# A four-layer sequence model on one Trainium2 core: layer 3 moved into the list scheduler, and bank-to-SBUF moves on whichever engine is free

## The chip, the core and the metric

The kernel runs on one core of one Trainium2 chip. The core has a matrix engine (PE, with its weight loads listed apart as PEld), three elementwise engines (DVE, ACT, POOL) and a sync engine (SP) that issues most DMAs. Each engine works through its own queue in order; the engines wait for each other by semaphores. On-chip data lie in SBUF; PE writes its results to PSUM, which has eight banks of 128 x 512 float32 values, and DVE or ACT read them from there. The metric is the device time of one execution in microseconds, lower being better.

## The reference, cut to what matters

A batch of two sequences of 1024 tokens with 256 features goes through four layers, each adding to x. Layer 0 is a linear attention. Layers 1 and 2 are state-space layers: layer 1 has one recurrence, layer 2 two (the second one runs over the reversed sequence). Layer 3 is a full softmax attention of 16 heads of 16 features.

```python
# layer 1 (layer 2 has two of these, the second on the flipped sequence)
dA  = exp(dt[:, :, None] * A)                  # 512 channels x 16 states
hst = hst * dA + (dt * x)[:, :, None] * B[:, None, :]
y   = einsum('bds,bs->bd', hst, C)
...
# layer 3
xn = layer_norm(x); q = xn @ q_w + q_b; k = xn @ k_w + k_b
att = softmax(einsum('bnhl,bmhl->bnmh', q, k) + (1 - mask) * -1e6, axis=2)
v = (xn @ v_w + v_b) * mask
y = einsum('bnmh,bmhl->bnhl', att, v)
h = layer_norm(y) * (1 + scale) + shift        # scale, shift from emb
return x + silu(h) @ out_w + out_b
```

## The kernel before, in words

**Layer 0** runs first, one batch after the other, with the framework's own scheduling. It is not changed, but for the pool of two small tiles.

**Layers 1 and 2** are made of twelve *halves*: 3 recurrences x 2 batches x 2 halves of 512 tokens. A half is 64 scans: 16 states x 4 blocks of 128 channels, numbered 64 * i + 4 * s + m. For each scan,

- ACT scales `dtuT` to `bxT` (line 774, `scaled`) and makes the decay `da` = exp(dt * a) (L788, `decay`);
- PE transposes four 128x128 blocks of `bxT` into a PSUM bank (L603 in `four`, called from `turned`);
- DVE runs the scan itself over `da` and that bank into `state` (L822, `scan`);
- POOL multiplies the state with a row `cb` spread over partitions (L854, `weighted_state`), into one of four `hc` buffers;
- PE transposes `hc` and sums it in four accumulation banks (L869, `summed`), which `drained` (L883) copies out at the end of a half, two on DVE and two on ACT.

Around the recurrences lie chains that prepare the next halves and finish the last: `before_1`, `step_sizes`, `between`, `before_2`, `after_1`, `after_2a`, `after_2b`, `joined`. They use PE products (`project` L608, `out_rows` L617), PSUM banks that they hold for some operations, and 42 SBUF buffers of 128x512 called `unit`.

Who comes next is not left to the framework in this stage. A *list scheduler* in Python (class `Order`) runs while the kernel is built. Each chain is a generator, a *part*, that yields "this operation takes engine X for so long, and needs these results". The scheduler keeps planned times of every engine, picks the operation that can start earliest (ties go by a place number `v`, the scan's number or a chain's own), and only then lets the part emit its instruction. Buffers come from *stores* in the same way: `stores.banks` holds four PSUM banks for transposes and chains (of which chains may hold two at a time, by two *tickets*), `stores.acc` the four accumulation banks, and each buffer carries the planned time from which it is free. The durations are constants in `act`, `vec`, `gps`, `turn`, `mat`. The order found in this way is the order of each engine's queue (`manual_schedule` over PE, ACT, DVE, POOL, SP). The semaphore waits are added by the framework, from what the emitted instructions read and write.

The eight PSUM banks are eight tiles before:

```python
tiles = [mm.tile([P, TH], F32, name=f"bank{i}") for i in range(8)]
stores.acc = Store(order, tiles[:4])
stores.banks = Store(order, tiles[4:])
```

**Layer 3** opens after the scheduler is done, with its own pools and with PE alone in a written order. It loads x3 from HBM (`x_sb`), which `after_2b` wrote, loads the weights, normalises and transposes (L264), makes V (L299) and q, k (L1283). Eight groups follow, each four heads of one batch. A group has two passes. The *first pass* (`maxima`) makes scores (L1301, 32-row matmuls into pairs of banks `s`) and takes negated row maxima on DVE (L1305), which are put into q (L1311 to L1321). The second (`weighted`) makes the transposed scores (L1360, into three banks `ps`), takes exp on ACT (L1365), and sums p times V on PE (L1330 into `av`); at the end of a half of the queries `av` is copied, turned and divided (L1337 to L1345). The first pass of group n + 1, the second of group n and the projections of group n + 2 are woven together in 16 steps per group (`together`). The first group's first pass and the last group's second pass run without a partner. `modulated_out` (norm, silu, output product) follows after each batch's last group.

Of the kernel before, what the change touches and what calls it, by code (L numbers as in the profile page):

```python
# [10 lines left out]
F32 = mybir.dt.float32  # L11
# [10 lines left out]
P = 128  # L22
B, T, D = 2, 1024, 256
NB = T // P
# [153 lines left out]
def blocks_kernel(ctx: ExitStack, tc: tile.TileContext, d: dict, out: bass.AP, offs: dict):  # L178
# [255 lines left out]
    def layer0(b):  # L434
# [60 lines left out]
        qmax = small.tile([P, nh], F32, name="qmax")  # L495
# [3 lines left out]
        qsum = small.tile([P, nh], F32, name="qsum")  # L499
# [44 lines left out]
    def act(*needs, n=1, v=None):  # L544
        return op(ACT, 0.6 * n, 0.6 * n + 0.2, *needs, v=v)
# [7 lines left out]
    def turn(*needs, v=None):  # L553
        return op(PE, 0.64, 0.85, *needs, v=v)

    def mat(n, *needs, v=None):
        return op(PE, 0.925 * n, 0.925 * n + 0.2, *needs, v=v)
# [29 lines left out]
    def free_units(bufs, at):  # L587
        for b in bufs:
            stores.units.put(b, at)

# [69 lines left out]
    def step_sizes(H, w_dbc, w_dt, t_u, v0):  # L660
# [42 lines left out]
        def sizes(m):  # L703
# [30 lines left out]
            t1 = yield act(t1, H.dtuT)  # L734
            nc.scalar.copy(
                H.dtuT.tile[:, :, m * P : (m + 1) * P], b.tile.rearrange("p (k e) -> p k e", k=4)
# [12 lines left out]
    def recurrences(halves):  # L749
# [131 lines left out]
        def drained(a, y, k, t):  # L881
            t = yield (vec if k % 2 else act)(a, y, t)
            (nc.vector.tensor_copy if k % 2 else nc.scalar.copy)(y.tile, a.tile)  # L883
            stores.acc.put(a, t)
# [46 lines left out]
    def before_1(H, b, h, carry, v0):  # L931
# [14 lines left out]
        for kb in range(2):  # L946
            p = yield from bank()
            t = yield turn(p, *ts)
            four(p.tile, lambda k: block_of(xg, k)[:, kb * P : (kb + 1) * P])
            t = yield act(t, hT[kb])  # L950
            nc.scalar.activation(
                hT[kb].tile, p.tile, AF.Identity, bias=bm[:, kb, b : b + 1], scale=wm[:, kb, b : b + 1]
            )
            free_bank(p, t)
# [4 lines left out]
        def convolved(m):  # L959
# [5 lines left out]
            t1 = yield act(t1, x)  # L965
            nc.scalar.copy(raw[:, 3:], p.tile)
            t1 = yield op(ACT, 0.3, 0.5, t1)
# [3 lines left out]
            else:  # L971
                nc.scalar.copy(raw[:, :3], carry[:, m, :])
            t1 = yield act(t1)
            nc.scalar.activation(
                p.tile, p.tile, AF.Identity, bias=col("conv_b", m), scale=cw(m, 3)
            )
# [9 lines left out]
        def gates():  # L986
            for m in range(NM):
# [3 lines left out]
                t1 = yield act(t1, z[m])  # L991
                nc.scalar.copy(z[m].tile, p.tile)
# [45 lines left out]
    def between(b, h, v0):  # L1038
# [46 lines left out]
        for kb in range(2):  # L1085
# [3 lines left out]
            t = yield act(t, xT[kb])  # L1089
            nc.scalar.activation(  # L1090
                xT[kb].tile, p.tile, AF.Identity, bias=col("norm2_b", kb), scale=col("norm2_g", kb)
# [6 lines left out]
        def activation():  # L1098
            z = yield get(stores.units, NM)
            for m in range(NM):  # L1100
# [3 lines left out]
                t1 = yield act(t1, z[m])  # L1104
                nc.scalar.activation(z[m].tile, p.tile, AF.Identity, bias=col("bx", m))
# [13 lines left out]
    def joined():  # L1119
# [5 lines left out]
        for i, name in enumerate(("w2b", "w2c")):  # L1125
# [4 lines left out]
            for m in range(2):  # L1130
# [7 lines left out]
                t2 = yield act(t2)  # L1138
                nc.scalar.copy(wz[:, i, m, :], b.tile)
# [18 lines left out]
    def before_2(H, b, i, h, v0):  # L1158
# [5 lines left out]
        for m in range(NM):  # L1164
# [3 lines left out]
            t = yield act(t, H.u[m])  # L1168
            u = H.u[m].tile
            nc.scalar.activation(  # L1170
                u[:, ::-1] if i else u, p.tile, AF.Identity,
                bias=bzc[:, i * NM + m : i * NM + m + 1],
# [24 lines left out]
    def after_2b(H, b, h, v0):  # L1197
# [39 lines left out]
        free_units(H.u, t1)  # L1237


    def attention_inputs(b):  # L1240


        xb = x_sb[:, b * NB : (b + 1) * NB, :]
        xn = work.tile([P, NB, D], F32, name="xn", tag="t8")
        layernorm(xn, xb, NB)
        xT = work.tile([P, 2, T], F32, name="xT", tag="t8")
        to_features(xn, affine(xT, lambda kb: col("norm_w", kb), lambda kb: col("norm_b", kb)))


        mrow = work.tile([1, T], F32, name="mrow3", bufs=1)  # L1250
        nc.scalar.dma_start(mrow, d["mask_rows"][1, b : b + 1, :])
        nc.vector.tensor_scalar(mrow, mrow, -1.0, 1.0, ALU.mult, ALU.add)
        nc.vector.tensor_scalar(mrow, mrow, -1e6, None, ALU.mult)
        mrow_d = dram.tile([1, T], F32, name="mrow_d")
        nc.sync.dma_start(mrow_d, mrow)

        vp = vps[b]

        def evac_v(t, ps):
            tmp = work.tile([P, 2, D], F32, name="res", bufs=2)  # L1260
            nc.vector.tensor_tensor(tmp, ps, over(bv3, 2), ALU.add)
            for j in range(2):
                c = (B + b) * NB + t + j
                nc.gpsimd.tensor_scalar(
                    vp[:, t + j, :, :HD3],
                    tmp[:, j, :].rearrange("p (h e) -> p h e", e=HD3),
                    mcols[:, c : c + 1], None, ALU.mult,
                )

        linear_t(view(w3b, 0, 2, D), xT, 2, evac_v)  # L1270
        y = work.tile([P, NB, D], F32, name="y3", bufs=2)
        return xT, mrow_d, vp, y

    def queries_and_keys(xT, mrow_d, g, out):

        q = work.tile([P, T], F32, name="q3", bufs=3)
        k = work.tile([P, T], F32, name="k3", bufs=3)
        out.append((q, k))
        for dst, w, name in ((k, 2 * E, "k_b"), (q, 0, "q_b")):
            for h in range(2):  # L1280
                ps = mm.tile([P, TH], F32, name="ps")
                for kb in range(2):
                    nc.tensor.matmul(  # L1283
                        ps, lhsT=view(w3a, w, 2, E)[:, kb, g * P : (g + 1) * P],
                        rhs=xT[:, kb, half(h)], start=kb == 0, stop=kb == 1,
                    )
                nc.scalar.activation(dst[:, half(h)], ps, AF.Identity, bias=col(name, g))
                yield
        for j in range(4):
            r = 32 * j + HD3 + 1  # L1290
            nc.sync.dma_start(k[r : r + 1, :], mrow_d)

    def maxima(q, k, negm, half_max):

        for t in range(NB):
            for h in range(2):
                for jp in range(2):
                    s = scp.tile([P, 2, TH], F32, name="s")
                    for i in range(2):
                        r = slice(64 * jp + 32 * i, 64 * jp + 32 * i + 32)  # L1300
                        nc.tensor.matmul(  # L1301
                            s[:, i, :], lhsT=q[r, t * P : (t + 1) * P], rhs=k[r, half(h)],
                            start=True, stop=True,
                        )
                    nc.vector.tensor_reduce(  # L1305
                        half_max[:, h, t, 2 * jp : 2 * jp + 2], s, AX.X, ALU.max, negate=True
                    )
                    yield
            if t % 4 == 3:
                h, ts = t // 4, slice(t - 3, t + 1)  # L1310
                nc.vector.tensor_tensor(  # L1311
                    negm[:, ts, :, HD3], half_max[:, 0, ts, :], half_max[:, 1, ts, :], ALU.min
                )
                ps = mm.tile([P, TH], F32, name="ps")
                for i in range(4):
                    nc.tensor.transpose(
                        ps[:, i * P : (i + 1) * P],
# [400 lines left out]
```

## Time and profile before

| what | value |
|---|---|
| median of 3 runs | 2410.27 us (2406.91 to 2411.26) |
| profiled execution, its own time | 2412.0 us |
| profiled execution, span from first to last instruction | 2410.2 us |
| mean granted PE clock | 0.947 |
| PE busy | 2027.8 us, 84% of the span |
| DVE busy | 1626.6 us, 67% |
| ACT busy | 1620.8 us, 67% |
| POOL busy | 1167.9 us, 48% |
| first and last scan start | 296.8 and 1639.6 us |
| first score matmul of layer 3 | 1699.4 us |

The shares are averages over stages: layer 0 up to 297 us, the twelve halves up to 1641, layer 3 after that. So the profile is read stage by stage, with the table of busy times by stretch, and within a stage by what ended the idle time of an engine (the waits). A wait is written "engine tile line <- engine tile line: total us, times, longest". An engine's row "128x512 f32 x768 | 553.8, 725" is the number of instructions, their busy time together and the mean ns of one. Matmuls of float32 count twice or more in such rows, since one is issued as several passes; four 128x128 transposes make one "turn".

### The profile page before, as it was taken

To read this page: it belongs to the slowest core of one execution; us is meant where nothing else is said; L and a number is where in the kernel's file an instruction comes from. 1 tells how busy PE (TensorE), PEld (TensorE's weight loads), DVE (VectorE), ACT (ScalarE), POOL (GpSimd) and SP (SyncE) were. 2 spreads that over 40 slices of the span, in tenths; PEclk is the share of its full clock that TensorE was granted. 3 is DMA by queue.
4 is the path that set the end of the run, shared out by engine and by line. 5 is a ranking of instruction groups with operands and counts; after the bars stand their busy time and mean duration, and the time that the engine had idled before them with its cause. 6 is when DMAs were issued, how large, how long until landed. Compare 5 with 4: busy or idle time off the path is not lost.

```text
span 2410.2 us, 32499 instructions
## 1 busy us (share of the span) xinstructions
PE 2027.8 (84%) x11648; PEld 1237.1 (51%) x11648; DVE 1626.6 (67%) x1958; ACT 1620.8 (67%) x2738; POOL 1167.9 (48%) x1022
## 2 busy tenths in 40 slices
PE   5766788988888788887888888885899999899986
PEld 4555456666666566656666666664343233323322
DVE  2462368797978787988887897995655555555622
ACT  1223689798979799998897898982034454445544
POOL 1012259595978787979777797995110000000000
PEclk9887799999999999999999999997889999999989
DMA  5002122122212321223131211323000000000000
GB/s 224 0 18 70 40 50 67 58 61 62 80 62 68 82 55 53 71 54 110 58 93 50 62 47 55 86 65 124 1 1 1 1 1 1 18 1 1 1 1 18
DMA packets 119898, 118.71 MB, mean 49 GB/s; under 512 B 59348, under 2 KB 78164, under 8 KB 118840
## 3 DMA queue, kind: packets, MB, share of 16 engines
q1 hardware_dynamic: 116612, 109.63, 15.3%
q0 software_dynamic: 1536, 4.20, 0.5%
q10 hardware_dynamic: 1588, 2.80, 0.4%
q8 instruction: 92, 1.51, 0.3%
q14 instruction: 70, 0.57, 0.1%
HBM read 92.92 MB, written 23.47 MB: 48 GB/s over the span
## 4 chain that ended last, share of the span: by engine, by line
PE 37%; ACT 11%; DVE 8%; POOL 7%; issue 3%; DMA 1%; POOLq 0%; DVEq 0%; SPq 0%; ACTq 0%
PE ps L1360 9%; PE s L1301 7%; POOL hc L854 6%; PE av L1330 5%; DVE state L822 5%; ACT da L788 4%; ACT bxT L774 4%; PE ps L1283 3%; PE bank L869 3%; PE bank L603 2%; PE bank L608 2%; DVE half_max L1305 1%; PE bank L617 1%; PE ps L299 1%; PE bank L668 1%
## 5 line engine op out<-in xcount | busy, mean ns | idle before, releaser
L854 POOL TENSOR_TENSOR hc<-state,cb 128x512 f32<-128x512 f32 x768 | 959.5, 1282 | 236.9 <-DVE state L822 199.8
L869 PE MATMUL bank<-ident,hc 128*128 128x128 f32 x3072 | 496.8, 286 | 151.5 <-POOL hc L854 95.9
L788 ACT ACTIVATE da<-unit,a_neg 128x512 f32<-128x512 f32 x768 | 553.8, 725 | 61.6 <-DVE state L822 60.9
L774 ACT ACTIVATE bxT<-dtuT,bT 128x512 f32<-128x512 f32 x768 | 546.7, 724 | 16.3 <-PE bank L603 15.8
L822 DVE TENSOR_TENSOR_SCAN state<-da,last,bank 128x512 f32<-128x512 f32 x384 | 468.2, 1266 | 59.0 <-PE bank L603 44.1
L869 PEld LDWEIGHTS bank<-ident,hc 128*128 128x128 f32 x3072 | 339.3, 143 | 325.3 <-POOL hc L854 286.2
L822 DVE TENSOR_TENSOR_SCAN state<-da,bank 128x512 f32<-128x512 f32 x384 | 451.8, 1209 | 80.6 <-PE bank L603 34.9
L603 PE MATMUL bank<-ident,bxT 128*128 128x128 f32 x3072 | 464.3, 278 | 32.7 <-DVE state L822 24.4
L1305 DVE TENSOR_REDUCE half_max<-s 128x2 f32<-128x1024 f32 x256 | 303.1, 1220 | 214.6 <-PE ps L1360 185.4
L1365 ACT ACTIVATE p<-ps 128x512 f32<-128x512 f32 x512 | 278.8, 597 | 250.4 <-PE ps L1360 247.1
L603 PEld LDWEIGHTS bank<-ident,bxT 128*128 128x128 f32 x3072 | 361.5, 143 | 80.5 <-DVE state L822 43.5
L1360 PE MATMUL ps<-q,k 32*128 32x512 f32 x1024 | 365.3, 644 | 8.2 <-ACT p L1365 8.1
L319 POOL TENSOR_TENSOR x_sb<-x_sb,res 128x512 f32<-128x512 f32 x16 | 20.5, 1284 | 672.1 <-DVE res L317 672.1
L1301 PE MATMUL s<-k,q 32*128 32x512 f32 x1024 | 277.3, 655 | 8.0 <-DVE half_max L1305 7.8
L1360 PEld LDWEIGHTS ps<-q,k 32*128 32x128 f32 x1024 | 115.3, 186 | 137.7 <-ACT p L1365 98.4
L1301 PEld LDWEIGHTS s<-k,q 32*128 32x128 f32 x1024 | 90.2, 192 | 140.2 <-DVE half_max L1305 94.7
L1330 PE MATMUL av<-p,vp 128*32 128x512 f32 x1024 | 137.7, 615 | 0.0
L603 PE MATMUL bank<-ident,unit 128*128 128x128 f32 x448 | 74.4, 299 | 14.9 <-POOL unit L730 5.3
L730 POOL TENSOR_TENSOR unit<-unit,unit 128x512 f32<-128x512 f32 x48 | 61.2, 1276 | 33.0 <-DVE unit L726 33.0
L274 ACT ACTIVATE xT<-ps,cols 128x512 f32<-128x512 f32 x16 | 11.5, 775 | 92.9 <-PE ps L264 92.8
L1330 PEld LDWEIGHTS av<-p,vp 128*32 128x32 f32 x1024 | 21.2, 109 | 94.2 <-issue 93.3
L603 PEld LDWEIGHTS bank<-ident,unit 128*128 128x128 f32 x448 | 55.3, 152 | 27.3 <-POOL unit L730 8.2
(194 smaller groups left out, 1957.5 us busy)
## 6 DMA issues: line engine op xcount, KB each, us to landing
cb<-c_d SPq DMA_DIRECT2D x192, 256.0 KB
sz_d<-unit SPq DMA_DIRECT2D x16, 256.0 KB
unit<-sz_d SPq DMA_DIRECT2D x16, 256.0 KB
x_d<-unit SPq DMA_DIRECT2D x16, 256.0 KB
act_d<-unit SPq DMA_DIRECT2D x16, 256.0 KB
y_d<-unit SPq DMA_DIRECT2D x16, 256.0 KB
unit<-y_d SPq DMA_DIRECT2D x16, 256.0 KB
unit<-act_d SPq DMA_DIRECT2D x16, 256.0 KB
```

The source lines that it names most:

```text
L603: nc.tensor.transpose(ps[:, k * P : (k + 1) * P], src(k), ident)
L774: nc.scalar.activation(x.tile, H.dtuT.tile[:, k, :], AF.Identity, scale=H.bT.tile[:, k * 2 * NS + s : k * 2 * NS + s + 1],)
L788: nc.scalar.activation(x.tile, H.dt[m].tile, AF.Exp, scale=a_neg[:, H.n, m, s : s + 1])
L822: nc.vector.tensor_tensor_scan(st.tile[:, m % 2, :], da.tile, bx.tile, H.last[:, s, m : m + 1] if H.h else 0.0, ALU.mult, ALU.add,)
L854: nc.gpsimd.tensor_tensor(x.tile, st.tile[:, m % 2, :], c.tile, ALU.mult)
L869: nc.tensor.matmul(acc[k].tile[:, m * P : (m + 1) * P], lhsT=x.tile[:, k * P : (k + 1) * P], rhs=ident, is_transpose=True, start=s == 0 an ...
L1283: nc.tensor.matmul(ps, lhsT=view(w3a, w, 2, E)[:, kb, g * P : (g + 1) * P], rhs=xT[:, kb, half(h)], start=kb == 0, stop=kb == 1,)
L1301: nc.tensor.matmul(s[:, i, :], lhsT=q[r, t * P : (t + 1) * P], rhs=k[r, half(h)], start=True, stop=True,)
L1305: nc.vector.tensor_reduce(half_max[:, h, t, 2 * jp : 2 * jp + 2], s, AX.X, ALU.max, negate=True)
L1330: nc.tensor.matmul(av[32 * j : 32 * j + 32, :], lhsT=vp[:, t, 4 * g + j, :], rhs=p[j], start=t == 0, stop=t == NB - 1,)
L1360: nc.tensor.matmul(s, lhsT=k[r, t * P : (t + 1) * P], rhs=q[r, half(h)], start=True, stop=True,)
L1365: nc.scalar.activation(p[j], s, AF.Exp)
```

## The change

1. Layer 3 becomes parts of the scheduler: `keys_mask`, `attention_inputs`, `queries_and_keys`, `steps`, `sums_of`, `shift`, `finished`, `attention_out`. Batch 0's inputs and the first q and k have places in the last half (`step0 - 60`, `step0 - 40`, where `step0` = 768 is the place after the last scan). The steps themselves begin in `freed`, when the last half's accumulation banks are drained. Its buffers are the units and the other stores' buffers, given back there. x3 is read from HBM in quarters, again at the end for the residual.
2. The planner treats PE's four 32-row groups as four resources in these steps (`_start`), and an operation may name several engines: `moved` offers a bank-to-SBUF move to ACT (0.52) or DVE (0.68), and emits it for the one that the planner took.
3. The planned durations of `act`, `turn` and `mat` change.
4. The eight banks are four tiles of two banks each, so that a pair can be reduced by one instruction in layer 3; the stores hold their halves.
5. A store serves waiting parts in the order of their places.

```diff
     def act(*needs, n=1, v=None):
-        return op(ACT, 0.6 * n, 0.6 * n + 0.2, *needs, v=v)
+        return op(ACT, 0.615 * n, 0.615 * n + 0.2, *needs, v=v)
...
     def turn(*needs, v=None):
-        return op(PE, 0.64, 0.85, *needs, v=v)
+        return op(PE, 0.45, 0.8, *needs, v=v)
...
     def mat(n, *needs, v=None):
-        return op(PE, 0.925 * n, 0.925 * n + 0.2, *needs, v=v)
+        return op(PE, 0.87 * n, 0.87 * n + 0.25, *needs, v=v)
...
+    def moved(dst, p, *needs, scale=None, bias=None):
+        src = p if isinstance(p, bass.AP) else p.tile
+        t = yield "op", None, [(ACT, 0.52, 0.7), (DVE, 0.68, 0.8)], None, [
+            n.at if isinstance(n, Buf) else n for n in needs
+        ], None
+        if order.took == ACT:
+            if scale is None and bias is None:
+                nc.scalar.copy(dst, src)
+            else:
+                kw = {k: v for k, v in (("scale", scale), ("bias", bias)) if v is not None}
+                nc.scalar.activation(dst, src, AF.Identity, **kw)
+        elif scale is not None:
+            nc.vector.tensor_scalar(dst, src, scale, bias, ALU.mult, ALU.add)
...
     def drained(a, y, k, t):
-            t = yield (vec if k % 2 else act)(a, y, t)
-            (nc.vector.tensor_copy if k % 2 else nc.scalar.copy)(y.tile, a.tile)
+            t = yield from moved(y.tile, a, a, y, t)
             stores.acc.put(a, t)
...
+    def steps(groups):
+        behind = []
+        last = len(groups) - 1
+        for n in range(-1, len(groups)):
...
+            for i in range(2 * NB):
+                v = step0 + 16 * n + i
+                yield "at", v
+                h, t = i // NB, i % NB
+                if n >= 0:
+                    if t == 0:
+                        ready = max((yield wait(shifted[n, h])), (yield wait(vp_done[b])))
+                        (av,) = yield get(stores.banks)
+                    ps = yield get(stores.units, 4)
+                    ends = []
+                for jp in range(2):
+                    if n < last:
+                        (x,) = yield get(stores.pairs)
+                        for j in range(2):
+                            t1 = yield op(2 * jp + j, 0.88, 1.15, need, x)
+                            r = slice(64 * jp + 32 * j, 64 * jp + 32 * j + 32)
+                            nc.tensor.matmul(
+                                x.tile[:, j, :],
+                                lhsT=q1[i // 8].tile[r, (i // 2 % 4) * P : (i // 2 % 4 + 1) * P],
+                                rhs=k1[i % 2].tile[r, :], start=True, stop=True,
+                            )
+                        seen.append(
+                            order.part(reduced(x, hm[:, i % 2, i // 2, 2 * jp : 2 * jp + 2], t1, v), v)
+                        )
+                    if n >= 0:
+                        for j in (2 - 2 * jp, 3 - 2 * jp):
+                            (x,) = yield get(stores.banks)
+                            t1 = yield op(j, 0.88, 1.15, ready, x)
+                            r = slice(32 * j, 32 * j + 32)
+                            nc.tensor.matmul(
+                                x.tile, lhsT=k0[t // 4].tile[r, (t % 4) * P : (t % 4 + 1) * P],
+                                rhs=q0[h].tile[r, :], start=True, stop=True,
+                            )
+                            ends.append(order.part(weights(x, ps[j], t1, v), v))
...
+                if n >= 0:
+                    behind.append((b, g, h, t, ends, ps, av))
+                    if len(behind) > 2:
+                        yield from sums_of(*behind.pop(0))
...
+    def freed():
+        groups = [(b, g) for b in range(B) for g in range(NG)]
+        yield wait(halves[-1].y_done)
+        acc = yield get(stores.acc, 4)
+        for t in tiles[:2]:
+            stores.pairs.put(Buf(t), max(x.at for x in acc))
...
-                tiles = [mm.tile([P, TH], F32, name=f"bank{i}") for i in range(8)]
-                stores.acc = Store(order, tiles[:4])
-                stores.banks = Store(order, tiles[4:])
+                tiles = [mm.tile([P, 2, TH], F32, name=f"bank{i}") for i in range(4)]
+                banks = [t[:, j, :] for t in tiles for j in range(2)]
+                stores.acc = Store(order, banks[:4])
+                stores.banks = Store(order, banks[4:])
+                stores.pairs = Store(order, [])
...
+    def _start(self, eng, at):
+        s = max(at, self.engine.get(eng, 0.0))
+        if isinstance(eng, int):
+            return max(s, self.engine.get(PE, 0.0))
+        if eng == PE:
+            return max([s] + [self.engine.get(r, 0.0) for r in range(4)])
+        return s
```

The moves that become `moved` are those of `step_sizes` (`dtuT`), `before_1`, `between`, `before_2`, `joined` and `drained`. In the changed kernel the lines of the same operations are: transposes L623, `bxT` L794, `da` L808, scan L842, `hc` L874, sums L889, first-pass scores L1426, second-pass scores L1439, p times V L1460, maxima L1476, exp L1499, moves L599 and L602 on ACT and L604 to L608 on DVE.

## The prediction

> **What bounds the kernel now.** I read the page's slices first, then the busy time by stage, then the waits of the long stage, then the timeline of single steps. Lines named before 1714 are the kernel's before unless "after" stands beside them.
>
> ```profile
> PE   5766788988888788887888888885899999899986
> DVE  2462368797978787988887897995655555555622
> ACT  1223689798979799998897898982034454445544
> POOL 1012259595978787979777797995110000000000
> ...
> 297.00:1641.00 1344.00, 1150.83 (x7265) 846.16 (x7265) 1124.01 (x1170) 1207.02 (x2020) 1083.00 (x944) 0.98 0.24 67
> 1641.00:1701.00 60.00, 36.77 (x134) 24.94 (x133) 28.84 (x79) 7.44 (x14) 26.37 (x21) 0.74 0.24 80
> 1701.00:1773.00 72.00, 62.34 (x204) 24.77 (x202) 42.95 (x41) 5.70 (x8) 4.83 (x6) 0.72 0.00 0
> 1773.00:2313.00 540.00, 505.56 (x2939) 170.78 (x2936) 306.69 (x363) 265.95 (x480) 7.46 (x7) 0.99 0.01 3
> 2313.00:2384.00 71.00, 61.93 (x263) 15.96 (x261) 4.10 (x19) 35.98 (x65) 0.00 (x0) 0.86 0.00 0
> 2384.00:2410.00 26.00, 12.15 (x55) 9.60 (x52) 9.33 (x30) 6.36 (x9) 5.06 (x4) 0.79 0.12 41
> ```
>
> The second block is the busy table by stretch (stretch, length, then PE, PEld, DVE, ACT, POOL, granted clock, DMA share, GB/s). Layers 1 and 2 run from 297 to 1641 with four engines at 81 to 90%: no single engine bounds them, the interlocking of their orders does. Layer 3 is a PE stage (94% in its seven full groups), behind a hole of 60 us in which x3 goes through HBM and layer 3's inputs are made.
>
> ```profile
> DVE state L822 <- PE bank L603: 79.0, 39, 6.3
> ACT da L788 <- DVE state L822: 60.9, 58, 6.8
> ...
> PE bank L603 <- DVE state L822: 25.0, 60, 2.4
> ```
>
> These are waits of that long stage (total us, times, longest). The scan waits for its transposed input in only 39 of 768 cases: with four separate PSUM tiles of one bank each, PE fills ahead of the scan. This is the cover that the change touches.
>
> **The change part by part.** I set the built order of both programs, with what each instruction waits for, side by side.
>
> *Layer 3's lead-in.* x3 of batch 0, layer 3's weights, its norm, V and the first q/k go into the last half (scan index 704 to 768); batch 1's go into the first groups. The 60 us hole shrinks to the last products and copies: scans end at 1641 and the last hc product at 1644.4, so about 5. The first pass of group 0 then has 32 reduces x 1.22 (row L1305) = 39, with after_2b's DVE work (4 x (0.74 + 0.67) + 4 x 0.70 = 8) and two shifts (2 x 0.9) on the same queue, plus 3 of handovers: 52 instead of 72.
>
> *Seven full groups.* The timeline of a step without projection (1934.01 to 1937.92) gives 3.9 us: 112 x 3.9 = 437. q/k of five groups, 20 x 1.92 (L1283, four matmuls) = 38; 28 sets of four transposes x 0.65 = 18; batch 1's transposes and V, moved in here, 2.6 + 7.4 = 10; batch 0's output the same, 10. Before, 540 held 437 + 46 + 18 + 11 and 28 of stalls. The planner hides those stalls; what it brings is below (50). Sum 563.
>
> *Last group and tail.* The last group keeps three banks for scores, so 71 stays about 70. The tail loses the first half's norm but loads x3 again: each later load stands behind the preceding output on SP, and waits with it for DVE. Three loads in a row at 2.7 (the like load at 1660.64 to the add at 1663.47) less cover: 26 becomes 32. The 64 small mask DMAs (32 before) ride on a queue that has room (DMA share 0.00 to 0.01 in that stage). Layer 3 in all: 769 becomes 5 + 52 + 563 + 70 + 32 = 722, **-47**. In the last half the added work (PE about 20, ACT and DVE about 8 each) meets ACT at 42 of 100 us after 1600: **+5**. The eight mask operations on POOL (nearest row: memset, 0.95) fit into its 261 idle us.
>
> *Moves on either engine.* In the built order 70 moves go to DVE where 24 did; 46 x 0.59 = 27 come off ACT and 46 x 0.68 = 31 go onto DVE (rows L883: ACT 590 ns, DVE 681). ACT is the fuller engine (90 against 84%), so I take **-15** together with the better durations (a run of transposes costs 0.44 per four, 1458.04 to 1459.35, where the old plan had 0.64); bounds -40 and +10.
>
> *PSUM tiles of two banks.* This is what the diff alone hides. `bank0..7` [128x512] become `bank0..3` [128x2x512], and the built order now waits by tile: a transpose into one half waits for the scan that reads the other half, and the reverse. Comparing each wait with the last instruction that touches the same half, layers 1 and 2 hold about 470 waits of PE for DVE and 380 of DVE for PE that the data does not need, and 106 ACT on PE, some 117 more ACT on DVE, 86 more DVE on ACT. The planner knows none of them. Behind a waiting turn on PE stand the sums of hc (L889 after), which free POOL's four hc buffers; behind a waiting scan, every other DVE link of the preparing chains.
> For the scan: where PE's turn waits for scan k, and scan k+1 waits for the turns behind it, nothing overlaps. Four transposes span 0.60, each further one adds 0.11, two handovers 0.11 each (1920.12 to 1920.23, 1920.89 to 1921.00): 0.82 + 0.11 x (n - 4), less 1.21 for each DVE instruction in between. Over the 768 scans this sums to 119 us in the new order (76 with nothing in between, 173 with one) and 30 in the old (9 and 65): **+89**. For the others: ACT on PE 106 x 0.3 + ACT on DVE 117 x 0.6 (half a scan) + DVE on ACT 86 x 0.35 + DVE's other instructions on PE 130 x 0.3 = 171; half of it I put on the path, since every engine idles 10 to 19% there: **+86**. Lower bound 0 (a wait can't speed anything, and all may lie in slack); upper: 380 x 0.82 + 171 = 483. I stay at 175, near the row that I have: the old sum of 30 stands beside 79 measured, so the count runs low rather than high.
> The same in layer 3: about 20 score matmuls wait for an exp that itself waits for the matmul just before (20 x 0.9), 40 av sets wait for such an exp (40 x 0.4), and for 2.3 steps of each half-group two av banks are held (the next is taken at its first step, the old one copied two steps on), leaving two for scores (14 x 2.3 x 0.5): the 50 above.
>
> [...] Physically the kernel still rotates through the same four banks. [...]
>
> **Sum**, against the profiled execution's own 2412.0 (span 2410.2 and 1.8 around it): 2412 + 89 + 86 - 15 + 5 - 47 = 2530. The median of the three runs is 1.7 lower, 2410.3; so 2528.
>
> **The rivals.** (1) *The waits lie in slack: faster.* In the steady second part of nine of the twelve halves the scans take both halves of one tile, then both of the other; there a turn has two scans (2.4 us) for 1.7 us of transposes and handovers, which loses nothing. If the disturbed first parts are as lenient, because ACT bounds them, layers 1 and 2 change by -15 and the kernel takes about 2355. It decides at 0.075 us per scan: above 57 us over 768 scans the gain of layer 3 is gone. For it: 220 idle us on DVE. Against: three halves alternate between the tiles, and in the disturbed parts two or three of the four half tiles carry all scans. (2) *The waits compound.* A late scan delays ACT's decay and POOL's product, whose orders are fixed too (POOL already waits 199.8 us for scans). At twice the count, layers 1 and 2 lose 350: about 2700. (3) *Layer 3 serialises too*: if each score pair waits for both exps of its tile, a step takes 4.9 (the fourth score starts at 2.85, 1.05 for it, 1.0 for av), not 4.35, adding 112 x 0.55 = 62: about 2590.
>
> **How the numbers follow.** My sum with its spread (2450 to 2600): 0.50. Compounding, alone or with (3): 0.28. Waits in slack: 0.17, and a draw 0.01; 0.04 for partial absorption that still ends just faster. What a measurement can tell from no change is 0.2%, 5 us. So slower 0.78, same 0.01, faster 0.21. The range 2365 to 2690 leaves about a tenth out at each end; where it is slower, its own range is 2440 to 2690.
>
> **What would show it.** In the new profile: the scan's wait for PE's turns (after, L842 on L623) well above 79 us, over 150; new rows of ACT waiting for scans other than the decay's; layers 1 and 2 ending 160 us later, near 1800; first scores of layer 3 within 10 us of the last scan; no x_sb hole; full groups near 80 us each. I am wrong if the scans still end by 1700, or if the full groups grow past 95 us each.

## The result, and the profile after

The changed kernel takes 2805.95 us (median of 4 runs, 2792.98 to 2812.66) where the kernel before takes 2409.43 beside it: a ratio of 1.164 (95% interval 1.159 to 1.169). It is slower, as forecast, but by 397 us and not by 118, and outside the range.

The slices of the page after the change, and the same table by stretch as before (stretch, length, then PE, PEld, DVE, ACT, POOL busy, granted clock, DMA share, GB/s):

```profile
PE   6667677767777777767688887778999999999986
...
ACT  1223686775868588777588798862443434344432
...
PEclk9888788998899999999899999899889999899856
```

```profile
307.00:1912.00 1605.00, 1215.82 (x7332) 917.66 (x7330) 1172.93 (x1235) 1215.85 (x2004) 1095.77 (x974) 0.93 0.20 58
1912.00:1918.00 6.00, 4.41 (x24) 2.34 (x24) 1.44 (x3) 1.76 (x3) 3.77 (x5) 1.00 0.00 0
1918.00:1976.00 58.00, 52.23 (x206) 20.87 (x200) 44.49 (x45) 4.81 (x7) 9.64 (x20) 0.94 0.12 37
1976.00:2650.00 674.00, 640.42 (x2950) 225.78 (x2948) 310.32 (x365) 290.83 (x524) 5.76 (x28) 0.91 0.01 4
2650.00:2769.00 119.00, 107.89 (x277) 27.58 (x276) 6.43 (x23) 38.31 (x71) 1.44 (x7) 0.52 0.01 3
2769.00:2809.00 40.00, 18.48 (x70) 10.18 (x68) 9.15 (x22) 9.89 (x16) 1.44 (x7) 0.71 0.15 46
```

The span grew by 399 us. 10 of them lie ahead of the first scan (307 against 297), 261 in layers 1 and 2 (1605 against 1344), 128 in layer 3 (897 against 769). Two readings stand out. In the first row of the table all engines are less busy in share (ACT 76%, not 90), so no engine became the bound: every engine waits more. And the clock column fell in every long stage: 0.93 where it was 0.98, 0.91 where it was 0.99 in the seven full groups, and 0.52 where it was 0.86 in the last group, which took 119 us instead of 71. The hole in front of layer 3 is gone: first scores at 1917.2, 5 us after the last scan's end.

The waits that answer to those shown of before (engine line waited for: us in total, times, longest):

```profile
POOL hc L874 <- DVE state L842: 337.0, 206, 10.7
...
PE bank L623 <- DVE state L842: 171.1, 198, 2.6
...
DVE state L842 <- PE bank L623: 129.3, 105, 6.3
ACT da L808 <- DVE state L842: 122.9, 91, 7.1
```

The prediction shows three of the like waits of before; the fourth, POOL's, was:

```profile
POOL hc L854 <- DVE state L822: 199.8, 129, 14.3
```

PE's transposes waited 25.0 us for scans before and now wait 171.1; the scans waited 79.0 for transposes and now 129.3; ACT's decay waits for scans 2.0 times as long (60.9 before) and POOL's product 1.7 times. One stretch of the timeline shows how the scan and the turn wait for each other (a row is start, duration, instruction, and in brackets the engine's idle time before it and what ended that):

```profile
570.80 4.93 DVE L842 TENSOR_TENSOR_SCAN state<-da,last,bank 128x512 f32<-128x512 f32 x4 [0.85 <-PE bank L623]
...
575.79 0.66 PE L623 MATMUL bank<-ident,bxT 128*128 128x128 f32 x4 [1.59 <-DVE state L842]
...
576.58 1.28 DVE L842 TENSOR_TENSOR_SCAN state<-da,last,bank 128x512 f32<-128x512 f32 x1 [0.85 <-PE bank L623]
```

The four scans end at 575.73, the turn starts at 575.79, the next scan at 576.58: 0.85 us of idle DVE, where the prediction's formula for a turn that nothing covers said 0.82. PE had stood idle for 1.59 us before the turn, waiting for the scans.

### The profile page after: what moved, and what is told of

Read it like the earlier page. It is cut to its first block, busy times and chain, and to the rows that moved or that the text cites. A ratio compares the mean times of both kernels' runs of the same rounds, so it can differ in the third digit from the quotient of the medians.

```text
span 2809.1 us, 32717 instructions
## 1 busy us (share of the span) xinstructions
PE 2238.3 (80%) x11648; PEld 1347.0 (48%) x11648; DVE 1656.7 (59%) x1951; ACT 1652.5 (59%) x2764; POOL 1167.2 (42%) x1090
## 5 line engine op out<-in xcount | busy, mean ns | idle before, releaser
L874 POOL TENSOR_TENSOR hc<-state,cb 128x512 f32<-128x512 f32 x768 | 962.3, 1275 | 450.7 <-DVE state L842 337.0
L623 PE MATMUL bank<-ident,bxT 128*128 128x128 f32 x3104 | 515.5, 298 | 245.9 <-DVE state L842 147.7
L808 ACT ACTIVATE da<-unit,a_neg 128x512 f32<-128x512 f32 x768 | 545.5, 713 | 123.9 <-DVE state L842 122.9
L623 PEld LDWEIGHTS bank<-ident,bxT 128*128 128x128 f32 x3104 | 376.1, 151 | 371.7 <-DVE state L842 212.9
L842 DVE TENSOR_TENSOR_SCAN state<-da,last,bank 128x512 f32<-128x512 f32 x384 | 471.6, 1267 | 128.9 <-PE bank L623 66.1
L794 ACT ACTIVATE bxT<-dtuT,bT 128x512 f32<-128x512 f32 x768 | 539.3, 711 | 10.6 <-PE bank L623 10.3
L842 DVE TENSOR_TENSOR_SCAN state<-da,bank 128x512 f32<-128x512 f32 x384 | 450.5, 1207 | 152.7 <-PE bank L623 63.2
L889 PE MATMUL bank<-ident,hc 128*128 128x128 f32 x3072 | 484.4, 290 | 63.6 <-POOL hc L874 53.1
L1476 DVE TENSOR_REDUCE half_max<-bank 128x2 f32<-128x1024 f32 x256 | 306.9, 1220 | 305.5 <-PE bank L1439 158.1
L889 PEld LDWEIGHTS bank<-ident,hc 128*128 128x128 f32 x3072 | 380.6, 150 | 143.8 <-POOL hc L874 91.7
L1499 ACT ACTIVATE unit<-bank 128x512 f32<-128x512 f32 x339 | 193.4, 596 | 266.3 <-PE bank L1439 182.6
L1439 PE MATMUL bank<-unit,unit 32*128 32x512 f32 x384 | 166.8, 721 | 11.3 <-ACT unit L1499 5.4
L1426 PE MATMUL bank<-unit,unit 32*128 32x512 f32 x384 | 122.0, 716 | 5.8 <-DVE half_max L1476 5.8
L623 PE MATMUL bank<-ident,unit 128*128 128x128 f32 x512 | 89.4, 303 | 46.3 <-DVE state L842 23.4
L623 PEld LDWEIGHTS bank<-ident,unit 128*128 128x128 f32 x512 | 64.3, 154 | 76.4 <-issue 20.0
L1439 PEld LDWEIGHTS bank<-unit,unit 32*128 32x128 f32 x384 | 52.1, 206 | 61.3 <-ACT unit L1499 27.7
L599 ACT COPY unit<-bank 128x512 f32<-128x512 f32 x53 | 30.2, 586 | 83.0 <-PE bank L889 28.2
L1426 PEld LDWEIGHTS bank<-unit,unit 32*128 32x128 f32 x384 | 40.1, 210 | 69.3 <-issue 35.9
L1460 PE MATMUL bank<-unit,unit 128*32 128x512 f32 x368 | 71.2, 668 | 1.6 <-ACT unit L1499 1.4
L628 PE MATMUL bank<-unit,wz 128*128 128x512 f32 x128 | 64.7, 629 | 9.3 <-DVE state L842 5.7
```

Of the source, the lines that this page charges most:

```text
L623: nc.tensor.transpose(ps[:, k * P : (k + 1) * P], src(k), ident)
L628: nc.tensor.matmul(ps, lhsT=w[:, kb, at + m * P : at + (m + 1) * P], rhs=rhs[kb].tile, start=kb == 0, stop=kb == 1,)
L794: nc.scalar.activation(x.tile, H.dtuT.tile[:, k, :], AF.Identity, scale=H.bT.tile[:, k * 2 * NS + s : k * 2 * NS + s + 1],)
L808: nc.scalar.activation(x.tile, H.dt[m].tile, AF.Exp, scale=a_neg[:, H.n, m, s : s + 1])
L842: nc.vector.tensor_tensor_scan(st.tile[:, m % 2, :], da.tile, bx.tile, H.last[:, s, m : m + 1] if H.h else 0.0, ALU.mult, ALU.add,)
L874: nc.gpsimd.tensor_tensor(x.tile, st.tile[:, m % 2, :], c.tile, ALU.mult)
```

## The experiments

Stage lengths are in us, from the one profiled run of each kernel: layers 1 and 2 from the start of the first scan to that of the last, then the seven full groups, the last group, the tail (all rounded; the tables by stretch are cut at whole us and can differ by 1). Where an edit leaves layers 1 and 2 alone, their length repeats within a few us: 1330 to 1334 in e1, f2 and g1, 1604 to 1611 in the changed kernel, f1 and h2. Medians are of 4 runs each (f3 and g2: 6, e4: 20); ratios are to the kernel before, run beside them.

| kernel | median us | ratio, 95% interval | layers 1, 2 | full groups, clock | last group, clock | tail |
|---|---|---|---|---|---|---|
| before | 2409.43 | 1 | 1343 | 540, 0.99 | 71, 0.86 | 26 |
| after | 2805.95 | 1.164 (1.159 to 1.169) | 1604 | 674, 0.91 | 119, 0.52 | 40 |
| e1 one-bank tiles | 2383.75 | 0.986 (0.978 to 0.995) | 1330 | 564, 0.98 | 99, 0.62 | 37 |
| e2 before, two-bank tiles | 2708.15 | 1.124 (1.117 to 1.131) | 1624 | 540, 0.99 | 71, 0.88 | 26 |
| e3 = e1, fixed moves | 2377.42 | 0.986 (0.980 to 0.992) | 1331 | 573, 0.97 | 71, 0.93 | 36 |
| e4 = e1, old durations | 2411.14 | 1.000 (0.998 to 1.003) | 1367 | 566, 0.98 | 77, 0.84 | 36 |
| f1 = after, more scores | 2761.41 | 1.142 (1.136 to 1.149) | 1611 | 666, 0.93 | 78, 1.00 | 36 |
| f2 = e1, pairs given back | 2336.33 | 0.966 (0.960 to 0.971) | 1334 | 573, 0.97 | 44, 1.00 | 35 |
| f3 = e3, f2, early loads | 2327.93 | 0.964 (0.960 to 0.969) | 1332 | 563, 0.99 | 43, 1.00 | 29 |
| f4 = after, one pair fewer | 2602.81 | 1.076 (1.070 to 1.082) | 1470 | 642, 0.92 | 107, 0.57 | 37 |
| g1 = e1, late av bank | 2323.29 | 0.962 (0.957 to 0.966) | 1330 | 530, 1.00 | 69, 0.89 | 36 |
| g2 = f3, late av bank | 2293.20 | 0.950 (0.947 to 0.953) | 1334 | 530, 1.00 | 41, 1.00 | 28 |
| h1 = after, zero sums | 2829.11 | 1.174 (1.164 to 1.184) | 1620 | 667, 0.92 | 121, 0.52 | 39 |
| h2 = after, late av bank | 2779.53 | 1.150 (1.140 to 1.160) | 1604 | 654, 0.92 | 108, 0.58 | 37 |

### e1: the working banks as tiles of one bank

```diff
-tiles = [mm.tile([P, 2, TH], F32, name=f"bank{i}") for i in range(4)]
-banks = [t[:, j, :] for t in tiles for j in range(2)]
-stores.acc = Store(order, banks[:4])
-stores.banks = Store(order, banks[4:])
+tiles = [mm.tile([P, 2, TH], F32, name=f"bank{i}") for i in range(2)]
+stores.acc = Store(order, [t[:, j, :] for t in tiles for j in range(2)])
+stores.banks = Store(
+    order, [mm.tile([P, TH], F32, name=f"bank{i}") for i in range(2, 6)]
+)
```

> The changed kernel in the same order of instructions; only the four working banks are four PSUM tiles of one bank each again, the four accumulation banks stay two tiles of two (the maxima reduce a pair at once). Theory (the waits of two-bank tiles, and the low clock that the stalls bring): layers 1 and 2 fall from 1605 to about 1340, the scan's waits for PE's turns back to about 80 us; the seven full groups from 674 to 560 to 580, the last group from 118 to about 70; in all 2330 to 2390. Rival (the new order of the list scheduler is itself slower, and the tiles cost little): 2600 or more. Rival (the low clock of the last group has nothing to do with the tiles): the last group stays near 118 at a granted clock near 0.5, in all 2390 to 2440.

Each engine's instructions are the same as in the changed kernel, in the same order; only the waits differ. The table by stretch of e1:

```profile
291.00:1623.00 1332.00, 1134.58 (x7333) 867.34 (x7331) 1160.03 (x1235) 1196.06 (x2004) 1091.43 (x975) 0.97 0.24 70
...
1687.00:2251.00 564.00, 559.38 (x2958) 201.11 (x2956) 305.60 (x365) 290.61 (x525) 5.76 (x28) 0.98 0.02 5
2251.00:2350.00 99.00, 91.36 (x280) 23.17 (x276) 6.32 (x23) 38.22 (x73) 1.44 (x7) 0.62 0.01 3
```

The kernel takes 2383.75 us: 422 us come from four lines that move no instruction. Layers 1 and 2 get 273 us shorter and fall 12 below the kernel before; the full groups get 110 shorter. The last group stayed long at a low clock in this run, which leaves its cause open; e3, in nearly the same order, had 71 us at 0.93. Where the 273 us sit is read from DVE, the scans' engine. The two forms of the scan (busy, mean ns, then DVE's idle time just before them), first after, then e1:

```profile
L842 DVE TENSOR_TENSOR_SCAN state<-da,last,bank 128x512 f32<-128x512 f32 x384 | 471.6, 1267 | 128.9 <-PE bank L623 66.1
...
L842 DVE TENSOR_TENSOR_SCAN state<-da,bank 128x512 f32<-128x512 f32 x384 | 450.5, 1207 | 152.7 <-PE bank L623 63.2
```

```profile
L842 DVE TENSOR_TENSOR_SCAN state<-da,last,bank 128x512 f32<-128x512 f32 x384 | 469.2, 1268 | 37.6 <-PE bank L623 29.7
L842 DVE TENSOR_TENSOR_SCAN state<-da,bank 128x512 f32<-128x512 f32 x384 | 450.9, 1208 | 54.1 <-PE bank L623 22.9
```

DVE idles 432 us of the stage after (1605 - 1173) and 172 in e1, 260 more. 190 of them stand before scans (281.6 against 91.7). What the scans waited for in the changed kernel (us, times):

```profile
  PE bank L623: 129.3, 105
  PE bank L637: 25.4, 7
  PE bank L628: 20.1, 10
  PE bank L688: 15.1, 4
...
  PE bank L728: 10.1, 8
```

And in e1:

```profile
  PE bank L623: 52.5, 35
```

Turns account for 129.3 (52.5 in e1), 77 more. About 113 of the 190 are other waits. L628, L637, L688 and L728 are products of the preparing chains; the scans waited 70.7 us for them, and e1's list has none of these rows. A scan reads none of these products, and only the tiles differ between the two kernels: it waits for a product that is written into the other half of its tile. The remaining 70 us stand before DVE's other instructions.

### e2: the kernel before, with two-bank tiles

```diff
-tiles = [mm.tile([P, TH], F32, name=f"bank{i}") for i in range(8)]
+pairs2 = [mm.tile([P, 2, TH], F32, name=f"bank{i}") for i in range(4)]
+tiles = [t[:, j, :] for t in pairs2 for j in range(2)]
```

> The kernel before, with nothing changed but the tiles: the scheduler's eight banks are four tiles of two banks, in the same order of instructions. Layer 3 has its own pools and is untouched. Theory: the waits alone cost layers 1 and 2 what the change did, 200 to 270 us: 2610 to 2680, scans ending near 1870. Prediction's own size of this term, 175 less what is special to the new order: about 2550. Rival (it was the new order): within 20 us of 2410.

The row by stretch of layers 1 and 2, and the scans' wait for turns in it:

```profile
307.00:1933.00 1626.00, 1204.85 (x7276) 898.59 (x7274) 1141.99 (x1170) 1236.97 (x2021) 1091.43 (x946) 0.94 0.19 55
...
DVE state L822 <- PE bank L603: 154.9, 119, 6.3
```

The tiles alone cost the old order 281 us in layers 1 and 2, and 10 more ahead of the first scan (307 again): a little more than the new order. (Here the accumulation banks lie in pairs too; e1 leaves those of the changed kernel paired.) The rival of the new order falls. The scans' wait for turns rises by 76 us (154.9 against 79.0), nearly the same as from e1 to the changed kernel (77): in both orders this chain is little more than a quarter of the loss, and the rest lies in other waits.

### e3 and e4: the moves and the durations alone

e3 gives every move of layers 1 and 2 its engine of before; e4 keeps free moves and takes the old constants.

```diff
+def moved(dst, p, *needs, scale=None, bias=None, only=ACT):
...
+    ways = [(ACT, 0.52, 0.7), (DVE, 0.68, 0.8)]
+    t = yield "op", None, [w for w in ways if only in (None, w[0])], None, [
```

> e1 with the bank-to-SBUF moves of layers 1 and 2 fixed to their engines of before (ACT, and DVE for every second drained bank); layer 3's moves stay free. The prediction's -15 for moves and durations together: e3 10 us slower than e1. Rival (ACT does not bound the stage, DVE is as full): within 5 us of e1, or faster, since fewer moves wait in DVE's queue behind scans.

> e1 with the planned durations of before in act (0.6), turn (0.64, 0.85) and mat (0.925, +0.2); moves stay free. If the better durations bring a part of the predicted -15: 3 to 10 us slower than e1. Rival (the order's quality hangs on them little): within 5 us.

e3 equals e1 (stage 1331 and 1330): taking some 45 moves off the fuller engine (ACT has 2809 instructions in e3, 2764 in e1) brought nothing. e4's stage is 37 us longer than e1's, and its kernel 27, more than either theory allowed. So e1's 12 us below the kernel before are the 37 that the new durations gained in this order, less about 24 of something else in the change (layer 3's inputs, the stores' order by place, free moves under old durations). How that splits was not tried, nor whether other durations near these would do the same, since each set gives one order.

### f1: more PE work in the last group

```diff
+elif n == last:
+    if i == 0 and jp == 0:
+        spare = yield get(stores.pairs, 2)
+    for j in range(2):
+        yield op(2 * jp + j, 0.88, 1.15, ready, spare[jp])
+        ...
+        nc.tensor.matmul(spare[jp].tile[:, j, :], lhsT=k0[t // 4].tile[...], rhs=q0[h].tile[r, :], ...)
```

> The changed kernel with its two-bank tiles, and in the last group only, four more 32-row score matmuls per step on PE into the idle pair banks; nobody reads them. They add 16 x about 1.0 us of PE work at full clock, twice that at half. Theory (in the last group the clock sits at half because PE's load there is light; more load brings it back): the granted clock of the last group rises from 0.52 to near 1 and it takes 70 to 90 us instead of 119, in all about 2770. Rival (the clock does not depend on PE's load): it stays near half and takes 140 to 155, in all about 2835.

First what the last group looked like. Two of its steps in the changed kernel, then two of the kernel before, by the fourth score of each step:

```profile
2702.04 2.07 PE L1439 MATMUL bank<-unit,state 32*128 32x512 f32 x2 [0.41 <-ACT unit L1499]
...
2708.75 2.07 PE L1439 MATMUL bank<-unit,state 32*128 32x512 f32 x2 [0.77 <-ACT state L1499]
```

```profile
2346.53 1.12 PE L1360 MATMUL ps<-q,k 32*128 32x512 f32 x2 [0.67 <-ACT p L1365]
...
2350.38 1.12 PE L1360 MATMUL ps<-q,k 32*128 32x512 f32 x2 [0.67 <-ACT p L1365]
```

The same work (x2: a score is recorded as two matmuls), a like wait for ACT (0.41 and 0.77 against 0.67), and 6.71 us instead of 3.85 from step to step: a score takes 2.07 instead of 1.12. That is the clock (0.50 from 2656 to 2744), not a wait. f1's last group:

```profile
2653.00:2731.00 78.00, 72.66 (x416) 25.01 (x412) 4.43 (x19) 40.05 (x75) 1.44 (x7) 1.00 0.01 4
```

With more work it is 41 us shorter: the clock is 1.00 over the group, and the kernel is 45 us faster, all four runs (2758.7 to 2769.5) lying below the changed kernel's four. So more PE work kept the clock up here (1.00 against 0.52), shown for this stage only. It is not the only way: e3 and g1 have a last group of about 70 us at 0.93 and 0.89 without it.

### f4: one shared pair instead of two

```diff
-tiles = [mm.tile([P, 2, TH], F32, name=f"bank{i}") for i in range(4)]
+tiles = [mm.tile([P, 2, TH], F32, name=f"bank{i}") for i in range(3)]
 banks = [t[:, j, :] for t in tiles for j in range(2)]
+banks += [mm.tile([P, TH], F32, name=f"bank{i}") for i in range(3, 5)]
```

> The changed kernel in its order of instructions, but only two of the four working banks share a tile, the other two are tiles of their own (the accumulation banks stay as they are). The built waits: the serial chain scan, turn, scan sums to 46 us by the prediction's formula, against 119 with two pairs and 8 with none (e1). If the cost goes with that sum: the stage of layers 1 and 2 takes 1330 + 274 x 38/111 = 1424. If it goes with the number of shared banks: 1330 + 137 = 1467. Compounding (a few late scans delay everything): above 1500. Full groups of layer 3: half of the 111 us between e1 and the changed kernel, about 620.

Layers 1 and 2 of f4:

```profile
297.00:1769.00 1472.00, 1160.85 (x7334) 891.74 (x7335) 1166.33 (x1235) 1207.78 (x2004) 1094.94 (x975) 0.95 0.22 63
```

The stage takes 1470 us, where half the cost was 1467: in layers 1 and 2 the loss goes with the number of shared banks, at the three points tried (none, one pair, two pairs). It does not grow faster than that, as compounding would, and it does not follow the scan chain's sum (1424). The scans' wait for turns (DVE at L842 for PE at L623: 81.7 us, 71 times in f4's trace) has risen by 29 of the 77 us, 38%, near the sum's 34% (38 of 111), while the stage lost 51%: the sum was good for the chain, and the chain is not the stage. The full groups lost more than half of the 110 (642, 78 above e1).

### f2, f3, g1, g2: the rest of layer 3, and a better kernel

f2 gives half of each pair back when the last group begins; f3 is e3 with that and with x3's residual loads issued a group ahead; g1 and g2 take the bank of av when the first p times V is due.

```diff
+if n == last:
+    for x in (yield get(stores.pairs, 2)):
+        stores.banks.put(Buf(x.tile[:, 0, :]), x.at)
...
-    (av,) = yield get(stores.banks)
+    av = []
...
+    if t == 0:
+        av += yield get(stores.banks)
+    (av,) = av
     t1 = yield op(PE, 1.0, 1.25, t1, av)
```

> e1 with one half of each of the two pair tiles given to the working banks when the last group begins (it has no first pass any more): five to six banks instead of four, so that the fourth score need not wait for an exp. Last group: ACT's 64 exps x 0.6 = 38 or PE's 16 x (1.1 + 1.0) = 34 bound it, 40 to 50 us instead of 71 at full clock and 99 in e1; in all about 2340. Rival (the clock falls to half all the same): 70 to 80, in all 2360 to 2370.

> e3 (moves fixed) with f2's banks and x3's residual loads issued ahead, after the last but one group of the batch: the tail's three late loads (2.7 to 3.0 each) go. Theory: last group 40 to 50, tail 36 becomes 27 to 30; in all 2330 to 2345. Rival (the loads lie beside the products): as f2.

> e1 with the bank for av taken when the first p times V of the half is due, not at the half's first scores two steps earlier, so that two av banks are held at once no longer. The prediction put 14 x 2.3 steps x 0.5 = 16 us on this in its 50 for the full groups. Theory (that term holds): the seven full groups fall from 564 to about 548, in all about 2368. Rival (the stalls of some steps, 4.4 us instead of 3.9, come from the planner's order of PE, not from banks): groups within 5 us of 564.

> f3 with the late av bank of g1. If the term holds: about 2312. If not: within 5 us of f3's 2328.

```profile
1687.00:2217.00 530.00, 528.97 (x2960) 188.18 (x2958) 304.64 (x365) 286.44 (x525) 5.76 (x28) 1.00 0.02 5
2217.00:2286.00 69.00, 61.66 (x280) 17.07 (x280) 6.06 (x21) 37.92 (x72) 1.44 (x7) 0.89 0.01 4
```

```profile
1691.00:2221.00 530.00, 528.95 (x2962) 188.68 (x2958) 304.61 (x363) 286.20 (x525) 5.81 (x28) 1.00 0.02 7
2221.00:2262.00 41.00, 41.00 (x276) 13.14 (x276) 5.82 (x21) 34.37 (x69) 1.45 (x7) 1.00 0.00 1
```

The first block is g1, the second g2. The early av bank cost 34 us (564 to 530), twice the 16 put on it. With more banks the last group is PE without a gap (41.00 of 41). The early loads took 7 off the tail (36 in e3, 29 in f3). g2, at 2293.2 us, is 5.0% faster than the kernel before (0.947 to 0.953): moving layer 3 into the scheduler was sound. The free moves in layers 1 and 2 have no part in that, since g2, like e3, fixes them.

### h1 and h2: the clock in layers 1 and 2, and av beside two-bank tiles

```diff
+if 0 < 4 * s + m < 4 * NS - 1:
+    for k in range(2):
+        nc.tensor.matmul(acc[k].tile[:, m * P : (m + 1) * P], lhsT=zeros, rhs=ident,
+                         is_transpose=True, start=False, stop=False)
```

> The changed kernel with two more 128x128 transposes of a zero tile behind each set of four that sums hc (not the first and last of a half), added into the same accumulation banks, so that the sums stay as they are. That is 744 x 0.22 = 164 us of PE work in the stage of layers 1 and 2, where PE sat idle 390 of 1605 us. Theory (in that stage too, the stalls cost clock, and the low clock lengthens the serial chain; more PE work restores it): granted clock from 0.93 to 0.96 or more, and the stage no longer than 1605, perhaps 1560. Rival (the clock there costs little): the stage grows by 30 to 160.

> The changed kernel with its two-bank tiles, and the late av bank of g1. The late bank gave 34 us in the seven full groups with one-bank tiles (564 to 530). Theory (the two terms add): 674 becomes about 640, in all about 2770. Rival (most of the 110 us between e1 and the changed kernel came through the av bank held early, whose tile also holds a bank of scores): below 600. Rival (bound by the tile waits): still within 10 us of 674.

Layers 1 and 2 of h1:

```profile
302.00:1924.00 1622.00, 1311.79 (x8817) 1050.36 (x8816) 1174.34 (x1235) 1217.25 (x2004) 1098.03 (x974) 0.96 0.21 57
```

h1's clock rose from 0.93 to 0.96 as the theory said, but the stage grew by 16 us; PE was busy 96 us longer and still idles 310. The result lies between the theory (no longer than 1605) and the rival (30 or more longer): what the clock gave back, if anything, was less than what the added work cost. So what the low clock costs in layers 1 and 2 stays open. h2 gained 20 us in the full groups (674 to 654), less than the 34 by which the two terms would add, so the two do not simply add.

## Why the prediction was right in direction and wrong in size

Against the profiled execution the sum was 281 us short (2530, measured 2810.9): 10 ahead of the first scan, which it left out, 96 in layers 1 and 2, 175 in layer 3. Three of its steps failed: half of the waits outside the scan chain was left off the path (97 us short), the bank waits of the full groups were sized too small (most of 111 us), and the granted clock had no term at all (49 us in the last group, and a part of the other stages that stays open).

- **The mechanism** was right: waits by tile, hidden from planner and diff. e1 takes those of the working banks away and is faster than before (0.978 to 0.995), e2 adds such waits alone and is slower. The time of the first rival, 2355, comes near e1 (2384), whose working banks are tiles of their own; for two banks in one tile it does not hold (2806). It still has in it the 34 us that the full groups were given for tile waits; without them it is 2321.
- **The scan chain, +89:** measured 77 (129.3 - 52.5). Right, down to the single gap (0.85, formula 0.82).
- **The other waits, +86:** the first step that failed. They were counted at 171, and half was put on the path because every engine idles 10 to 19%. Measured as idle time of DVE that e1 does not have: 113 before scans plus 70 before DVE's other instructions, 183. (With the chain's 77 and 13 of longer busy time of DVE this is the 273 of e1.) The count was near and the halving was wrong: the idle 10 to 19% took up far less than half of the new waits. The likely reason, not tested apart, is that this idle time was itself made of waits in the same orders. Two limits: the four parts of the count were not measured one by one, and the 183 hold what the clock cost. If all of the stage scaled with the clock (0.97 in e1, 0.93 after), it would be 1292 against 1493 at full clock, an estimate from the two rows: about 200 of the 273 at least are waits, up to 70 clock. Even then some 120 (200 less the chain's 77) are left for these waits, where 86 were taken.
- **Moves and durations, -15, and layer 3's inputs, +5:** together -12 in e1. That the sum holds is luck: the moves gave nothing (e3), the durations 37 (e4), and some 24 of unknown origin stand against them.
- **Lead-in 5 and first pass 52:** 6 and 58 after, 7 and 57 in e1.
- **The seven full groups, 563:** measured 674, the second step that failed. The base of 513 for steps and projections was 17 short (530 in g1), the two av banks cost 34 instead of 16 (20 beside two-bank tiles, h2), the tiles 110 instead of 34 (124 from g1 to h2). That e1 shows 564 is luck. Within the 110 the granted clock fell from 0.98 to 0.91: if all of the stage scaled with the clock, it would be 553 against 613 at full clock, an estimate from the two rows: at least 60 are waits and up to 50 are clock. How they split within these bounds stays open.
- **The last group, "stays about 70":** 119 at a clock of 0.52; f1 takes 78 at 1.00 with more work in it, so some 41 or more of the 49 are the clock. The sum had no term for the clock anywhere; this is the third step that failed. What decides on the clock was not found.
- **The tail, 32:** 40 after, 37 in e1. The loads behind each other cost 7 (f3), near the 6 by which the tail was to grow.

The rivals: (1) that the waits lie in slack falls with e2. (2) Compounding (about 2700) comes nearest in time, but its 350 us for layers 1 and 2 were too many (274), and f4 shows no growth beyond the number of shared banks: that it comes nearest is luck. (3) A serial layer 3 (625 for the full groups) was too mild. Of the signs named beforehand, first scores within 10 us of the last scan and no hole came true, and so did ACT's new waits for scans (15.3 us before L602, 12.6 before L734); the scans' wait for turns above 150 was missed (129.3), and layers 1 and 2 end at 1912, not near 1800. The sign that the prediction is wrong came true as well: full groups past 95 us each (96.3).

## What to carry to other kernels

Where waits are made per tile, the shape of a tile is part of the schedule (281 us in layers 1 and 2 of e2): compare the built waits with the data that they protect. Where in-order engines bound a stage together and none bounds it alone, take the whole count of false waits as the first estimate; here about all of it came back as time (171 counted, 183 found), the clock's share included. A quick test is the same order with smaller tiles. And a PE stage costed at full clock needs a second price at a lower one: the last group here took 119 us at 0.52, and 78 at 1.00 with more work.

## What was not expected of the hardware

The clock can stay at half under steady matmul work. In the changed kernel's last group it was 0.50 from 2656 to 2744, although PE is busy for all of the first 8 us of this and for 71.84 of the 80 us from 2660 to 2740, and no wait of PE is longer than 1.2:

```profile
2656.00:2664.00 8.00, 8.00 (x18) 2.56 (x18) 0.00 (x0) 2.50 (x5) 0.00 (x0) 0.50 0.00 0
```

```profile
PE bank L1439 <- ACT unit L1499: 5.1, 8, 1.2
```

In the kernel before, the last group began in the same way, and then came out of it. From 2345 to 2383 the same step ran at full clock with a smaller busy share (31.67 of 38 us):

```profile
2324.00:2332.00 8.00, 7.12 (x22) 1.20 (x16) 0.00 (x0) 2.36 (x5) 0.00 (x0) 0.50 0.01 2
```

At full clock (1.00 over the last group) were f1, with more 32-row matmuls per step, and f2, f3 and g2, with hardly a gap on PE (busy for 43.85 of 44, 42.85 of 43 and 41.00 of 41 us). Most of the clock is there without either: g1's last group has neither (61.66 of 69 us), and its clock was 0.89. Which measure of load decides was not found. The times of the kernel before go with its mean clock too: its 23 runs beside e1 to e4 go from 2401.4 us at 0.955 to 2429.4 at 0.941, which is 1.2%, where the prediction took 0.2% for what a measurement can tell from no change. Whether this is the same effect was not tried.
